# First layer's selective scans: one C product in four on GpSimd, state copies on ScalarE, the D term on TensorE

## The chip, the cores and the metric

The kernel runs on one core of a Trainium2 chip. A core has four compute engines: TensorE (PE in the profile, with its weight loads as PEld), VectorE (DVE), ScalarE (ACT) and GpSimd (POOL). SyncE (SP) computes nothing here; it issues DMA transfers between HBM and the on-chip memory SBUF. TensorE writes its results to PSUM, a second on-chip memory. Each engine runs its own queue in order and waits on semaphores for the others. The metric is the device time of one execution in microseconds, as a median over runs.

## What is computed

A two-layer vision network over 8 images of 128 channels x 64 x 64 positions. The change touches the mixer of the first layer alone. For each image it runs four selective scans ("mamba" blocks), one for each direction d in which the 4096 positions are read. For one direction, cut to what matters:

```python
def step(h, inp):
    x_t, dt_t, B_t, C_t = inp
    dA = jnp.exp(dt_t[..., None] * A)
    h = dA * h + (dt_t * x_t)[..., None] * B_t[:, None, :]
    y = jnp.einsum('bdn,bn->bd', h, C_t)
    return (h, y)
...
y = _selective_scan(xh, dt, A, Bm, Cm) + xh * Dp
y = y * jax.nn.silu(z)
return y @ out_w.T
```

Here h has 128 channels x 16 states. x, dt, B and C are made from the image by a small convolution, a gate and projections; the last two lines add the D term, apply the gate and project out. The four outputs are added to the image. After that come a token router with experts, and a second layer, which the change does not touch.

## The kernel before

**Tiling.** An image's 4096 positions are cut into four chunks of 1024 (`CH`) a direction: 16 chunks an image, 128 in all. The 128 x 16 states do not fit on 128 partitions, so a chunk is worked in 16 blocks (`NQ`): a block holds 8 channels x 16 states on 128 partitions and 1024 positions along the row. `scan_blocks` loops over all blocks n of an image and, in each turn, issues the work of several blocks at different stages:

- `dA` of block n+1: six bf16 matmuls spread dt (in three bf16 parts, tile `parts`) over the states into a PSUM tile (two buffers, tag `dA`); ScalarE turns it into exp(dt A) in place.
- `bx` of block n+1: GpSimd multiplies `xE` (dt x, spread over the states) by `B16`. Three buffers.
- `xE` of block n+3: SyncE issues a DMA which reads 8 rows of `dtx_d`, a copy of dt x in HBM, each row 16 times, and writes 128 partitions x 4 KB, 512 KB in all. Four buffers.
- the scan of block n on VectorE (line 622), from `dA` in PSUM and `bx` in SBUF, written over `dA`; then `hc`, the product with `C16`, on VectorE into SBUF; then the 1-column copy `last`, the state that the same block of the next chunk starts from (not in a direction's last chunk).
- once in four blocks, TensorE adds up the states of the four finished `hc` tiles into `y` in PSUM, half the row in each of two turns ("collects", 4 matmuls each).

**Steps.** What is done once a chunk, rather than once a block, stands in the table at the end of `scan_steps`. A row (at, step, ...) is issued at the end of turn 16 i + at of chunk i: -18 to -2 prepare a chunk while the one before is being scanned, 12 to 20 finish it. Of importance here: `lost` (-9, -8), `ln` and `dt` (-8, -7) make dt; `dtx` (-7, -6) multiplies by x on GpSimd and writes each half row to `dtx_d` by a DMA; `part` and `rest` (-6 to -2) make the three bf16 parts, the `rest` on GpSimd; `z_gate` and `gated` (13 to 16) make the gate `zs`; `skip` (17) adds the D term into `yt` on VectorE; `gate_y` (18, 19) multiplies by the gate on GpSimd, one half row at a time; `out_product` and `out_add` project and add to the image `r`.

**Order.** The helper `ordered` fixes every engine's order as the loop issues it, DMA issues apart: SyncE's order is made by the framework. It comes out as 15 `xE` of a chunk, `dtx` 0, one `xE`, `dtx` 1, then 15 `xE` of the next and so on. An `xE` of a chunk reads both half rows, so the first of them waits until both writes have landed. DMAs issued by SyncE share one queue and start in that order.

Of the kernel before, what the change touches and what calls it, by code (L numbers as in the profile page):

```python
# [9 lines left out]
F32 = mybir.dt.float32  # L10
BF16 = mybir.dt.bfloat16
AF = mybir.ActivationFunctionType
ALU = mybir.AluOpType
# [8 lines left out]
C = 128  # L22
L = 4096
S = 512
# [5 lines left out]
CH = 1024  # L30
# [3 lines left out]
NQ = C // 8  # L34
# [235 lines left out]
def bc(ap, n, axis=None):  # L270

    axis = len(ap.shape) if axis is None else axis
    v = ap.unsqueeze(axis)
    shape = list(v.shape)
    shape[axis] = n
    return v.to_broadcast(shape)


class Net:
# [154 lines left out]
    def scan_steps(self, ch, xp, r, pl, ps):  # L434
# [4 lines left out]
        nc, d, j = self.nc, ch["d"], ch["j"]  # L439
        pool = nc.gpsimd  # L440
# [3 lines left out]
        start = [lo + (1 - q if back else q) * S for q in range(2)]  # L444
        half = [slice(q * S, (q + 1) * S) for q in range(2)]
        ID, TANH = AF.Identity, AF.Tanh
        v = {}
# [4 lines left out]
        def bank(name):  # L452
            p = v[name] = ps.tile([C, S], F32, tag="m", bufs=2, name="m")
            return p

        def make(name, bufs, width=S):
            t = v[name] = pl.tile([C, width], F32, name=name.rstrip("01"), bufs=bufs)
            return t
# [80 lines left out]
                ch[name] = pl.tile([128, CH], F32, name=name, bufs=2)  # L539
            self.ordered(nc.scalar.copy(ch[name][:, half[q]], v[f"b{n}{q}"]))  # L540

        def skip():
            self.stt(make("yt", 1, CH), ch["xs"], self.w(f"D{d}"), ch["y"], ALU.mult, ALU.add)

        def gate_y(q):
            yt = v["yt"][:, half[q]]
            self.tt(yt, yt, v["zs"][:, half[q]], ALU.mult, pool)

        def out_product(q):
            self.mm(bank(f"o{q}"), self.Wo[:, d, :], v["yt"][:, half[q]])  # L550

        def out_add(q):
            p, lo = v[f"o{q}"], CH * j + q * S
# [18 lines left out]
            (-7, spread_copy, 0, 0), (-6, part, 0, 0), (-6, spread_copy, 0, 1), (-5, spread_copy, 1, 0),  # L572
            (-5, spread_copy, 1, 1), (-5, part, 0, 1), (-5, rest, 0, 0), (-4, rest, 0, 1), (-4, part, 1, 0),
            (-4, self.table, EXP_TANH_SET), (-3, part, 1, 1), (-3, rest, 1, 0), (-2, rest, 1, 1),
            (12, z_product, 0), (13, z_product, 1), (13, z_gate, 0), (14, z_gate, 1),
            (15, gated, v, "zs", 0), (16, gated, v, "zs", 1),
            (17, skip), (18, gate_y, 0), (19, gate_y, 1), (19, out_product, 0), (20, out_product, 1),
            (19, out_add, 0), (20, out_add, 1),
        ]
        return table  # L580

    def scan_blocks(self, xp, xt, r, pl, ps):

        nc = self.nc
        chunks = [{"d": d, "j": j} for d in range(4) for j in range(NCH)]
        todo = {}
        for i, ch in enumerate(chunks):  # L590
            for at, step, *args in self.scan_steps(ch, xp if ch["d"] < 2 else xt, r, pl, ps):
                todo.setdefault(NQ * i + at, []).append((step, args))
        total = NQ * len(chunks)
        self.order = {}
        self.table(EXP_TANH_SET)
        xE, bx, dA, hcs = {}, {}, {}, {}
        last = None
        for n in range(min(todo), max(todo) + 1):
            u = n + 1
            if 0 <= u < total:  # L600

                ch, q = chunks[u // NQ], 4 * (u % 4) + u % NQ // 4
                dA[u] = ps.tile([128, CH], F32, tag="dA", bufs=2, name="dA")
                sel = self.expand[:, 8 * q : 8 * q + 8, :].rearrange("p c n -> p (c n)")
                for h in range(2):
                    sg = slice(h * S, (h + 1) * S)
                    for i in range(3):
                        self.mm(dA[u][:, sg], sel, ch["parts"][:, i, sg], start=i == 0, stop=i == 2)
                self.act(dA[u], dA[u], AF.Exp, scale=self.negA[:, ch["d"] * NQ + q : ch["d"] * NQ + q + 1])
                bx[u] = pl.tile([128, CH], F32, name="bx", bufs=3)  # L610
                self.tt(bx[u], xE.pop(u), ch["B16"], ALU.mult, nc.gpsimd)
            u = n + 3
            if 0 <= u < total:
                ch, q = chunks[u // NQ], 4 * (u % 4) + u % NQ // 4
                xE[u] = pl.tile([128, CH], F32, name="xE", bufs=4)
                nc.sync.dma_start(xE[u], bc(ch["dtx"][8 * q : 8 * q + 8, :], NST, 1))
            if 0 <= n < total:
                ch, q = chunks[n // NQ], 4 * (n % 4) + n % NQ // 4
                if n % NQ == 0 and ch["j"] == 0:
                    last = pl.tile([128, NQ], F32, name="last", bufs=2)  # L620
                t = dA.pop(n)
                self.ordered(nc.vector.tensor_tensor_scan(  # L622
                    out=t, data0=t, data1=bx.pop(n), initial=0.0 if ch["j"] == 0 else last[:, q : q + 1],
                    op0=ALU.mult, op1=ALU.add,
                ))
                hcs[n] = pl.tile([128, CH], F32, name="hc", bufs=7)
                self.tt(hcs[n], t, ch["C16"], ALU.mult)
                if ch["j"] < NCH - 1:
                    self.copy(last[:, q : q + 1], t[:, CH - 1 :], nc.vector)
            if n % 4 < 2 and 4 <= n < total + 4:  # L630
                g0, h = n // 4 * 4 - 4, n % 4
                ch, k = chunks[g0 // NQ], g0 % NQ // 4
                if k == 0 and h == 0:
                    ch["y"] = ps.tile([C, CH], F32, tag="y", bufs=1, name="y")
                for g in range(4):
                    self.mm(ch["y"][32 * g : 32 * g + 32, h * S : (h + 1) * S], self.k("collect")[:, 32 * k : 32 * k + 32],
                            hcs[g0 + g][:, h * S : (h + 1) * S], start=k == 0, stop=k == 3)
                    if h:
                        del hcs[g0 + g]
            for step, args in todo.pop(n, ()):  # L640
                step(*args)
        self.order = None
        self.silus_done([])
# [1099 lines left out]
```

## Time and profile before

| | us |
|---|---|
| median of 3 runs | 20,433.81 |
| lowest and highest | 20,432.83 and 20,484.78 |
| span of the profiled execution | 20,491.5 |
| start of the first scan of image 0, of the last of image 7 | 128.8 and 9,602.4 |
| an image's scans, start of the first to start of the last | 1,046 to 1,067 |
| from there to the first scan of the next image | 142 to 145 |
| VectorE, GpSimd, ScalarE busy in 128 to 1,180 | 1,007.75, 815.29, 577.87 |
| TensorE busy in 128 to 1,180 | 791.13 |

The page gives the busy share of every engine over the span; the scans are its first 19 of 40 slices:

```profile
PE   7777677777777777777887888888888888888899
...
DVE  7989899898989989897354666666666666666886
ACT  5555555555555555554353555555555565555553
POOL 6767577676767767675011112112112112111444
...
DMA  4544454454435545444431000000000000001222
```

A digit is the busy share of a slice in tenths; for DMA it is the mean over the core's 16 DMA engines. A group's line in the profile reads: line of the code, engine, operation, tile written <- tiles read, shapes, count | busy us, mean ns of one | idle us of the engine just before them, and what ended it. Many operations have the line of a helper (330 for `tt`, 339 for `stt`, 288 for `mm`, 291 for `act`), so they are told apart by their tiles. In a waits list, "A <- B: us, times, longest" says that A's engine sat idle until B had finished. What bounds the kernel is read off in the prediction.

### The profile page before, as it was taken

What the parts mean: (1) busy time and instruction counts of PE and PEld (TensorE: products, weight loads), DVE (VectorE), ACT (ScalarE), POOL (GpSimd) and SP (SyncE); (2) the same over time, 40 slices, a digit from 0 to 9 for tenths busy, and PEclk for the clock granted to TensorE, in tenths of its full rate; (3) what the DMA queues carried; (4) which work ended last, traced back from release to release, by engine and by line L of the source; (5) the groups of instructions that cost most, each with busy time, mean ns of one, the idle gap of its engine ahead of it and who ended that gap; (6) DMA issues with size and microseconds to landing.
All of it is one profiled execution on the core that took longest, in us unless ns stands there. A gap on an engine that the chain in (4) does not pass through costs nothing. (4 is left out here: it accounts for less than half of the span.)

```text
span 20491.5 us, 295472 instructions
## 1 busy us (share of the span) xinstructions
PE 16535.8 (81%) x111237; PEld 8567.3 (42%) x112221; DVE 15704.4 (77%) x20825; ACT 11194.8 (55%) x15819; POOL 9136.4 (45%) x6292
## 2 busy tenths in 40 slices
PE   7777677777777777777887888888888888888899
PEld 2222222222222222222545666666666666665343
DVE  7989899898989989897354666666666666666886
ACT  5555555555555555554353555555555565555553
POOL 6767577676767767675011112112112112111444
PEclk9989999898999999898687999999999999999899
DMA  4544454454435545444431000000000000001222
GB/s 117 136 106 138 107 136 130 112 135 109 136 108 132 136 109 133 109 132 121 138 124 32 27 26 25 27 25 25 26 26 25 27 26 25 27 25 30 81 97 80
DMA packets 814160, 1684.21 MB, mean 82 GB/s; under 512 B 180859, under 2 KB 413211, under 8 KB 803803
## 3 DMA queue, kind: packets, MB, share of 16 engines
q1 hardware_dynamic: 812734, 1665.25, 29.0%
q8 instruction: 889, 14.57, 0.3%
q14 instruction: 537, 4.40, 0.1%
HBM read 1440.67 MB, written 224.26 MB: 81 GB/s over the span
## 5 line engine op out<-in xcount | busy, mean ns | idle before, releaser
L330 POOL TENSOR_TENSOR bx<-xE,B 128x1024 f32<-128x1024 f32 x2048 | 4819.4, 2354 | 1538.2 <-DMA xE<-dtx_d 1400.7
L288 PE MATMUL dA<-parts,expand 128*128 128x512 bf16 x11816 | 3180.0, 400 | 2124.9 <-DVE last L342 1551.1
L291 ACT ACTIVATE dA<-dA,negA 128x1024 f32<-128x1024 f32 x2048 | 2228.6, 1088 | 3731.3 <-PE dA L288 3647.5
L622 DVE TENSOR_TENSOR_SCAN dA<-dA,last,bx 128x1024 f32<-128x1024 f32 x1536 | 3611.2, 2351 | 209.7 <-POOL bx L330 200.9
L288 PEld LDWEIGHTS <-expand 128*128 128x128 bf16 x12288 | 1078.5, 100 | 4837.7 <-DVE last L342 2739.3
L291 ACT ACTIVATE E_cm<-ss_p 128x1024 f32<-128x1024 f32 x2048 | 1977.1, 1030 | 1545.7 <-PE ss_p L288 674.9
L339 DVE SCALAR_TENSOR_TENSOR E_cm<-E_cm,gm_cm 128x1024 f32<-128x1024 f32 x2048 | 2424.0, 1224 | 512.5 <-ACT E_cm L291 512.1
L330 DVE TENSOR_TENSOR hc<-dA,C 128x1024 f32<-128x1024 f32 x2048 | 2508.0, 1225 | 69.9
L1131 POOL COPY Sd_cm<-S_cm 64x128 f32<-64x128 f32 x1024 | 799.9, 781 | 2886.8 <-DVE S_cm L330 2753.9
L330 POOL TENSOR_TENSOR xD_cm<-tok_cm,D_cm 128x256 f32<-128x256 f32 x512 | 413.8, 808 | 2912.2 <-PE y_p L288 2791.1
L288 PE MATMUL y_p<-E_cm,pad_cm 128*32 128x128 f32 x32768 | 1388.7, 286 | 19.0 <-DVE E_cm L339 10.5
L288 PE MATMUL ss_p<-ssB_cm,ssA_cm 128*128 128x512 bf16 x3584 | 1178.8, 419 | 244.7 <-ACT E_cm L291 167.1
L622 DVE TENSOR_TENSOR_SCAN dA<-dA,bx 128x1024 f32<-128x1024 f32 x512 | 1173.6, 2292 | 197.5 <-POOL bx L330 196.3
L288 PE MATMUL y<-hc,kt 128*32 128x512 f32 x8192 | 1202.0, 652 | 37.8 <-DVE hc L330 31.6
L288 PEld LDWEIGHTS y_p<-E_cm,pad_cm 128*32 128x32 f32 x32768 | 939.4, 113 | 388.6 <-issue 240.7
L288 PE MATMUL bc_p<-stk_cm,W_cm 128*128 128x256 f32 x4096 | 1020.5, 392 | 25.9 <-DMA stk_cm<-xs 20.7
L330 DVE TENSOR_TENSOR gm_cm<-g_p,kt 128x1024 f32<-128x1024 f32 x512 | 624.2, 1219 | 506.3 <-PE g_p L288 501.4
L291 ACT ACTIVATE tok_cm<-tok_p 128x384 f32<-128x384 f32 x1024 | 502.3, 491 | 606.2 <-PE tok_p L288 450.9
L288 PEld LDWEIGHTS bc_p<-stk_cm,W_cm 128*128 128x128 f32 x4096 | 741.0, 191 | 197.0 <-issue 78.8
L291 ACT ACTIVATE BC_cm<-bc_p 128x1024 f32<-128x1024 f32 x512 | 524.9, 1025 | 539.6 <-PE bc_p L288 535.0
L288 PE MATMUL tok_p<-W_cm,stk_cm 128*128 128x200 f32 x4096 | 761.4, 339 | 0.0
L288 PE MATMUL g_p<-BC_cm 64*128 64x128 f32 x8192 | 743.2, 307 | 0.4
(391 smaller groups left out, 30156.3 us busy)
## 6 DMA issues: line engine op xcount, KB each, us to landing
xE<-dtx_d SPq DMA_DIRECT2D x2048, 512.0 KB
dtx_d<-dtx SPq DMA_DIRECT2D x256, 256.0 KB
pb<-p_d SPq DMA_DIRECT2D x64, 1024.0 KB
x<-x SPq DMA_DIRECT2D x192, 256.0 KB
ssA_cm<-cs_cm SPq DMA_DIRECT2D x3072, 4.0 KB
stk_cm<-xs SPq DMA_DIRECT2D x368, 128.0 KB
stk_cm<-y SPq DMA_DIRECT2D x368, 128.0 KB
x<-in_x_dram SPq DMA_DIRECT2D x64, 256.0 KB
```

Source lines behind the costliest of these rows:

```text
L288: self.ordered(self.nc.tensor.matmul(out, lhsT=lhsT, rhs=rhs, start=start, stop=stop))
L291: i = self.ordered(self.nc.scalar.activation(out, in_, func, **kw))
L330: self.ordered((eng or self.nc.vector).tensor_tensor(out, a, b, op))
L339: self.ordered(self.nc.vector.scalar_tensor_tensor(out=out, in0=a, scalar=s, in1=b, op0=op0, op1=op1))
L622: self.ordered(nc.vector.tensor_tensor_scan(out=t, data0=t, data1=bx.pop(n), initial=0.0 if ch["j"] == 0 else last[:, q : q + 1], op0=ALU. ...
L1131: nc.gpsimd.tensor_copy(Sd[gr, :, g * hi : (g + 1) * hi], S2[gr])
```

## The change

- `hc` of blocks 0, 4, 8 and 12 goes to GpSimd: VectorE's scan of block n writes into the SBUF tile `hc` instead of PSUM, and GpSimd multiplies it by `C16` in place in turn n + 1, behind bx of block n + 3.
- `last` is copied by ScalarE, in the scan's turn.
- `bx` is made two blocks ahead instead of one, with four buffers; `xE` is issued four blocks ahead instead of three, still with four buffers.
- The D term becomes eight fp32 matmuls on TensorE, with a diagonal weight `D_diag` (made once a direction), added to `y` in PSUM (16, 17).
- The gate is applied in one VectorE product, `y` in PSUM by `zs` into `zs`, instead of two on GpSimd. `yt` goes. `out_product` and `out_add` come one turn earlier.

In the built program SyncE's order becomes 16 `xE`, both `dtx`, 16 `xE`. On GpSimd the order around turns 9 to 14 becomes bx 11, hc 8, dtx 0, bx 12, dtx 1, bx 13, rest, bx 14, rest, bx 15, hc 12, rest, bx 0 of the next chunk, rest.

```diff
-        def skip():
-            self.stt(make("yt", 1, CH), ch["xs"], self.w(f"D{d}"), ch["y"], ALU.mult, ALU.add)
-
-        def gate_y(q):
-            yt = v["yt"][:, half[q]]
-            self.tt(yt, yt, v["zs"][:, half[q]], ALU.mult, pool)
+        def diagonal():
+            t = self.D_diag = pl.tile([C, C], F32, name="D_diag", bufs=1)
+            self.ts(t, self.k("ident"), self.w(f"D{d}"), ALU.mult)
+
+        def skip(q):
+            for g in range(4):
+                rows_ = slice(32 * g, 32 * g + 32)
+                self.mm(ch["y"][rows_, half[q]], self.D_diag[:, rows_], ch["xs"][:, half[q]], start=False)
+
+        def gate_y():
+            self.tt(v["zs"], ch["y"], v["zs"], ALU.mult)
 
         def out_product(q):
-            self.mm(bank(f"o{q}"), self.Wo[:, d, :], v["yt"][:, half[q]])
+            self.mm(bank(f"o{q}"), self.Wo[:, d, :], v["zs"][:, half[q]])
...
+            *([(12, diagonal)] if j == 0 else []),
             (12, z_product, 0), (13, z_product, 1), (13, z_gate, 0), (14, z_gate, 1),
             (15, gated, v, "zs", 0), (16, gated, v, "zs", 1),
-            (17, skip), (18, gate_y, 0), (19, gate_y, 1), (19, out_product, 0), (20, out_product, 1),
-            (19, out_add, 0), (20, out_add, 1),
+            (16, skip, 0), (17, skip, 1), (17, gate_y), (18, out_product, 0), (19, out_product, 1),
+            (18, out_add, 0), (19, out_add, 1),
...
-                bx[u] = pl.tile([128, CH], F32, name="bx", bufs=3)
-                self.tt(bx[u], xE.pop(u), ch["B16"], ALU.mult, nc.gpsimd)
-            u = n + 3
+            u = n + 2
             if 0 <= u < total:
-                ch, q = chunks[u // NQ], 4 * (u % 4) + u % NQ // 4
+                bx[u] = pl.tile([128, CH], F32, name="bx", bufs=4)
+                self.tt(bx[u], xE.pop(u), where(u)[0]["B16"], ALU.mult, nc.gpsimd)
+            u = n - 1
+            if 0 <= u < total and u % 4 == 0:
+                self.tt(hcs[u], hcs[u], where(u)[0]["C16"], ALU.mult, nc.gpsimd)
+            u = n + 4
+            if 0 <= u < total:
+                ch, q = where(u)
                 xE[u] = pl.tile([128, CH], F32, name="xE", bufs=4)
...
-                t = dA.pop(n)
+                a = dA.pop(n)
+                hcs[n] = pl.tile([128, CH], F32, name="hc", bufs=7)
+                t = a if n % 4 else hcs[n]
                 self.ordered(nc.vector.tensor_tensor_scan(
-                    out=t, data0=t, data1=bx.pop(n), initial=0.0 if ch["j"] == 0 else last[:, q : q + 1],
+                    out=t, data0=a, data1=bx.pop(n), initial=0.0 if ch["j"] == 0 else last[:, q : q + 1],
                     op0=ALU.mult, op1=ALU.add,
                 ))
-                hcs[n] = pl.tile([128, CH], F32, name="hc", bufs=7)
-                self.tt(hcs[n], t, ch["C16"], ALU.mult)
                 if ch["j"] < NCH - 1:
-                    self.copy(last[:, q : q + 1], t[:, CH - 1 :], nc.vector)
+                    self.ordered(nc.scalar.copy(last[:, q : q + 1], t[:, CH - 1 :]))
+                if n % 4:
+                    self.tt(hcs[n], t, ch["C16"], ALU.mult)
...
-                            hcs[g0 + g][:, h * S : (h + 1) * S], start=k == 0, stop=k == 3)
+                            hcs[g0 + g][:, h * S : (h + 1) * S], start=k == 0, stop=False)
```

More of the change, by code (lines that the diff above doesn't have):

```diff
@@ L594, in scan_blocks, with where @@
         self.order = {}
+        def where(u):
+            return chunks[u // NQ], 4 * (u % 4) + u % NQ // 4
         self.table(EXP_TANH_SET)
@@ L609, in scan_blocks @@
                 self.act(dA[u], dA[u], AF.Exp, scale=self.negA[:, ch["d"] * NQ + q : ch["d"] * NQ + q + 1])
-                bx[u] = pl.tile([128, CH], F32, name="bx", bufs=3)
-                self.tt(bx[u], xE.pop(u), ch["B16"], ALU.mult, nc.gpsimd)
-            u = n + 3
+            u = n + 2
             if 0 <= u < total:
-                ch, q = chunks[u // NQ], 4 * (u % 4) + u % NQ // 4
+                bx[u] = pl.tile([128, CH], F32, name="bx", bufs=4)
[5 more added lines that the diff above has]
+            if 0 <= u < total:
+                ch, q = where(u)
                 xE[u] = pl.tile([128, CH], F32, name="xE", bufs=4)
@@ L617, in scan_blocks @@
             if 0 <= n < total:
-                ch, q = chunks[n // NQ], 4 * (n % 4) + n % NQ // 4
+                ch, q = where(n)
                 if n % NQ == 0 and ch["j"] == 0:
                     last = pl.tile([128, NQ], F32, name="last", bufs=2)
-                t = dA.pop(n)
+                a = dA.pop(n)
+                hcs[n] = pl.tile([128, CH], F32, name="hc", bufs=7)
+                t = a if n % 4 else hcs[n]
                 self.ordered(nc.vector.tensor_tensor_scan(
-                    out=t, data0=t, data1=bx.pop(n), initial=0.0 if ch["j"] == 0 else last[:, q : q + 1],
+                    out=t, data0=a, data1=bx.pop(n), initial=0.0 if ch["j"] == 0 else last[:, q : q + 1],
                     op0=ALU.mult, op1=ALU.add,
                 ))
-                hcs[n] = pl.tile([128, CH], F32, name="hc", bufs=7)
-                self.tt(hcs[n], t, ch["C16"], ALU.mult)
                 if ch["j"] < NCH - 1:
-                    self.copy(last[:, q : q + 1], t[:, CH - 1 :], nc.vector)
+                    self.ordered(nc.scalar.copy(last[:, q : q + 1], t[:, CH - 1 :]))
+                if n % 4:
+                    self.tt(hcs[n], t, ch["C16"], ALU.mult)
             if n % 4 < 2 and 4 <= n < total + 4:
```

## The prediction

> **What bounds the kernel now.** The change touches only the scan stage of the first layer: 8 images of 16 chunks of 16 blocks, from 128.8 us to about 9,606 us of the span. I read the page's slices first (VectorE, DVE, at nine tenths there and the DMA engines at half), then the groups, the windows, the order in time of GpSimd (POOL), and the waits.
>
> ```profile
> L330 POOL TENSOR_TENSOR bx<-xE,B 128x1024 f32<-128x1024 f32 x2048 | 4819.4, 2354 | 1538.2 <-DMA xE<-dtx_d 1400.7
> L622 DVE TENSOR_TENSOR_SCAN dA<-dA,last,bx 128x1024 f32<-128x1024 f32 x1536 | 3611.2, 2351 | 209.7 <-POOL bx L330 200.9
> L330 DVE TENSOR_TENSOR hc<-dA,C 128x1024 f32<-128x1024 f32 x2048 | 2508.0, 1225 | 69.9
> ```
>
> VectorE looks like the bound: it idles only some 210 + 198 us before 2048 scans. But look at what GpSimd waits for: the copies xE, 1400.7 us. So to the DMA columns of the windows (last two: share of 16 engines, GB/s):
>
> ```profile
> 264.00:280.00 16.00, 12.75 (x50) 4.07 (x50) 15.86 (x15) 7.05 (x9) 13.80 (x8) 1.00 0.52 125
> 360.00:368.00 8.00, 4.66 (x19) 1.21 (x20) 7.93 (x7) 6.40 (x11) 5.67 (x3) 0.82 0.51 201
> 480.00:488.00 8.00, 6.01 (x25) 1.95 (x27) 7.93 (x8) 4.72 (x6) 7.59 (x5) 1.00 0.52 209
> 320.00:324.00 4.00, 3.93 (x16) 1.56 (x12) 3.96 (x4) 3.73 (x7) 2.59 (x3) 1.00 0.25 70
> ```
>
> The share stands at 0.51 to 0.52 whether 125 or 209 GB/s flow: a resource that is full at one half, whose packets sometimes go slowly, sometimes fast. A copy of 512 KB takes 524,288 B / 125 GB/s = 4.2 us in the one state, 2.5 us in the other. The same in time:
>
> ```profile
> 292.62 2.35 POOL L330 TENSOR_TENSOR bx<-xE,B 128x1024 f32<-128x1024 f32 x1 [1.85 <-DMA xE<-dtx_d]
> 296.82 2.35 POOL L330 TENSOR_TENSOR bx<-xE,B 128x1024 f32<-128x1024 f32 x1 [1.86 <-DMA xE<-dtx_d]
> 301.01 2.35 POOL L330 TENSOR_TENSOR bx<-xE,B 128x1024 f32<-128x1024 f32 x1 [1.84 <-DMA xE<-dtx_d]
> ...
> 329.48 2.37 POOL L330 TENSOR_TENSOR bx<-xE,B 128x1024 f32<-128x1024 f32 x1 [3.41 <-DMA xE<-dtx_d]
> ```
> ```profile
> 361.30 2.34 POOL L330 TENSOR_TENSOR bx<-xE,B 128x1024 f32<-128x1024 f32 x1 [0.32 <-DMA xE<-dtx_d]
> 363.93 2.35 POOL L330 TENSOR_TENSOR bx<-xE,B 128x1024 f32<-128x1024 f32 x1 [0.28 <-DVE hc L330]
> 370.01 1.26 POOL L330 TENSOR_TENSOR dtx<-dt,xs 128x512 f32<-128x512 f32 x1 [3.73 <-DVE dt L330]
> ```
>
> In the first, products start 4.20 us apart and each waits for its copy: the DMA paces all. The 3.41 us is a chunk's first copy, which cannot be issued before both writes of dtx have landed. In the second, GpSimd has caught up and stands at VectorE. So the stage swings between two limits. From the trace's DMA packets (128 of 4 KB a copy), chunk by chunk over all 128: a chunk takes 66.55 us on average (scan to scan, image ends apart); its 16 copies span 63.8, then come 2.7 idle to the next chunk's first packet. In only 29 chunks did the copies run out of buffers, because the engines were late. With those 29 closed up (copies after the stall at 2.6 us), I estimate 62.5 + 2.7 = 65.2 us a chunk for a DMA queue that nobody holds up. This is the floor.
>
> **What the Trainium skill says.** "DMA: Bandwidth & Descriptors", section "Why a DMA increments its semaphore by 16 and not by 1": a DMA is spread over as many engines as divide its slowest dimension, at most 16. Source of xE: 8 rows, each repeated 16 times; so 8 engines. The share of 0.51 agrees. "SBUF — State Buffer", "Two separate sides": compute cannot slow a DMA; agrees in that both rates occur with DVE above 90% busy. So no edit here speeds the copies. "Who interferes with whom" there: a VectorE instruction with one SBUF input does not contend with GpSimd. The changed ones (scan, gate_y) have the other in PSUM, and bx in the trace takes 2.35 us beside every VectorE operation; I keep all prices. "GPSIMD Engine Reference", "Elementwise": a two-input product costs GpSimd about twice VectorE's time; here 2354 to 1225 ns.
>
> **The change, part by part, for one chunk.** Durations overlap at their ends, so on VectorE I use start to start in its order of time (483.97, 486.35, 487.50, 487.56): scan 2.38, hc 1.14 to 1.15, last 0.07.
> VectorE before: 16 x (2.38 + 1.14 + 0.07) = 57.4; lost, m, dt twice each (0.60 + 0.72 + 0.61) = 3.9; yt 1.2; out_add 1.2 (2.0 or more where strided). Sum 63.7; chunks at this limit do take 62.7 to 64.5.
> - Four hc to GpSimd: -4 x 1.14 = -4.6.
> - last to ScalarE: -0.8. It costs ScalarE 12 x some 0.2 (as its 128x4 activation at 6.16 us) = 2.4; ScalarE is 55% busy. But the copy waits for the scan, and behind it in ScalarE's order stand the steps (plus_one, ln) which used to run during the scan.
> - yt to TensorE, and the gate from two GpSimd products to one VectorE product from PSUM: yt 1.18 against about 1.14: 0. TensorE gains 8 matmuls, 2 x 1.06 us (the price of four collects, each in two passes).
> - Bare sum -5.4: 58.3. New waits, each followed through the queues from one scan's end S: after a block whose C product is on GpSimd, VectorE goes straight to the next scan, but dA for it comes at S + 1.2 (hc) + 1.5 (six matmuls) + 1.1 (exp) + latencies = 3.95 against 3.55: 0.4, three or four times. In block 8 (no hc) lost waits for plus_one behind last: 1.5. gate_y in block 1 waits for dA, four collects and four skips on TensorE: 1.7. So -5.4 + 3.6 = -1.8: VectorE's chunk about 61.9 (bounds 58.3 and 63.7).
> - GpSimd: before 16 x 2.35 + 12 halves (10 + 2 gate_y) = about 52. After +4 x 2.35 - 2 x 1.23: 58.9. Also under the floor, but dense: blocks 9 to 14 carry six bx, two hc, two dtx and four rest, 25.8 us against 6 x 4.2 of DMA.
> - bx two ahead with four buffers, xE issued a block earlier with the same four: a copy still follows the release by bx of four blocks before, so the DMA's backlog (some 8 us, two copies) is the same. What moves is on SyncE: all 16 copies now precede both dtx writes, and dtx 1 comes behind bx 12 and hc 8 instead of bx 11 on GpSimd, some 6 us later against the copies. With copies at 4.2 us it is issued 7 us before copy 15 ends: hidden. Where the last four run at 2.5, the chunk's gap grows by about 2.1 us; I count this for one chunk in eight, 0.25 us.
> - Image ends: one block of steps less, gate in one product: -2 us, 8 times, -16.
>
> Sum. An infinitely fast consumer would give 66.55 - 65.2 = 1.35 us a chunk. VectorE at 61.9 instead of 63.7 gives about half of it: a chunk whose copies need 61 wins two thirds of its loss, one whose copies need 58 wins a third. -0.7 + 0.25 = -0.45 us, x 128 = -58, and -16: -74 us, on an execution of 20,491.5 us (the profiled one; the median of the runs shown is 57.7 lower). On the median 20,433.8: 20,360 us, -0.36%.
>
> **The rivals.**
> 1. The copies free of the engines: all of 1.35 is won, 128 x 1.35 + 16 = -189: 20,245. For it: VectorE's bare sum of 58.3. Against: the waits just counted.
> 2. VectorE bounds after all and -5.4 goes through: -691 - 16: 19,727. For it: its 0.9 busy. Against: share of 0.51 throughout.
> 3. No gain: the gap's growth of 2.1 us hits one chunk in three (0.7) and eats the win. Then only the -16 is left: 20,418.
> 4. Slower: the hold of the first copy by dtx. If GpSimd runs behind in blocks 9 to 14 (it has 0.9 us too much work there, and its hc waits for VectorE), dtx 1 is issued after copy 15 has ended, and every microsecond is DMA idle time. It decides from 7 us of lag at 4.2 us a copy, at once at 2.5. At 2 us in each chunk: +256, less the -74: 20,616.
> That the scans wait for PE's eight new matmuls, or bx 0 before the last rest delays the first dA (3 us once a chunk), is covered by the bx buffers while the DMA paces.
>
> **How the numbers follow.** Forecast 0.50, rival 1 0.15, rival 2 0.03, rival 3 0.17, rival 4 0.15. About 0.3% (61 us) is what a measurement can tell from no change; the three runs before differ by 52. Of the forecast's own range, 20,290 to 20,430, I put six tenths beyond -0.3%. Faster 0.30 + 0.15 + 0.03 = 0.48; same 0.20 + 0.17 = 0.37; slower 0.15. The range 20,230 to 20,520 leaves out rival 2, a little of rival 1 and most of rival 4.
>
> **What would show it.** Right: DMA share still 0.50 over an image's scans, GpSimd still waiting for xE, VectorE busy some 107 us less an image (16 x (4 x 1.225 + 12 x 0.148)) but idle in its place (more waits for bx, for sp_u and for y), hc on GpSimd at 2.35 us. Wrong: a mean packet rate that changed, products on VectorE or GpSimd that got longer, or SyncE waiting longer for dtx than the 976 us of before between 300 and 9,000 us.

## The result, and the profile after

| | before | after |
|---|---|---|
| median, same chip, 4 runs each | 20,435.16 us | 20,630.67 us |
| lowest to highest | 20,432.83 to 20,484.78 | 20,620.78 to 20,637.51 |
| span of the profiled execution | 20,491.5 us | 20,619.0 us |
| first scan of image 0 to last scan of image 7 | 9,473.6 us | 9,620.3 us |

The changed kernel is slower: ratio 1.0097, 95% interval 1.0081 to 1.0112, where 0.9964 was forecast. The profiled execution of before lies at the upper end of its runs, so the two spans differ by 127.5 us and the medians by 195.5; comparisons below use ratios of runs, and the profiles for the mechanism.

The same groups as shown of before, now of the changed kernel (128 to 9,790 us of the span):

```profile
L330 POOL TENSOR_TENSOR bx<-xE,B 128x1024 f32<-128x1024 f32 x2048 | 4811.4, 2354 | 833.4 <-DMA xE<-dtx_d 772.7 <-DVE dA L639 15.5 <-DVE hc L330 15.5
L639 DVE TENSOR_TENSOR_SCAN dA<-dA,last,bx 128x1024 f32<-128x1024 f32 x1152 | 2708.3, 2351 | 152.3 <-ACT last L644 105.1 <-ACT dA L291 44.2 <-POOL bx L330 2.9
L330 DVE TENSOR_TENSOR hc<-dA,C 128x1024 f32<-128x1024 f32 x1536 | 1881.1, 1225 | 775.0 <-ACT last L644 762.3
L330 POOL TENSOR_TENSOR hc<-hc,C 128x1024 f32<-128x1024 f32 x512 | 1208.2, 2360 | 93.6 <-ACT last L644 79.1 <-DVE hc L639 12.4 <-DMA xE<-dtx_d 1.8
```

No operation got dearer: bx still 2354 ns, the scan 2351, hc 1225 on VectorE and 2360 on GpSimd. GpSimd waits for copies half as long (772.7 us for 1400.7 us): the DMA paces less. What is new is in the third line. The C product used to follow its scan with 69.9 us of idle time in all; now 762.3 us pass, 1152 times, until ScalarE has copied `last`. The order in time of VectorE shows one block after another:

```profile
458.89 1.23 DVE L330 TENSOR_TENSOR hc<-dA,C 128x1024 f32<-128x1024 f32 x1 [0.23 <-ACT last L644]
460.03 2.29 DVE L639 TENSOR_TENSOR_SCAN dA<-dA,bx 128x1024 f32<-128x1024 f32 x1
462.89 1.23 DVE L330 TENSOR_TENSOR hc<-dA,C 128x1024 f32<-128x1024 f32 x1 [0.57 <-ACT last L644]
464.03 2.29 DVE L639 TENSOR_TENSOR_SCAN dA<-dA,bx 128x1024 f32<-128x1024 f32 x1
466.88 1.23 DVE L330 TENSOR_TENSOR hc<-dA,C 128x1024 f32<-128x1024 f32 x1 [0.57 <-ACT last L644]
```

and the same stretch of ScalarE why:

```profile
461.68 1.09 ACT L291 ACTIVATE dA<-dA,negA 128x1024 f32<-128x1024 f32 x1 [0.57 <-PE dA L288]
462.69 0.16 ACT L644 COPY last<-dA 128x1 f32<-128x1 f32 x1
...
465.67 1.09 ACT L291 ACTIVATE dA<-dA,negA 128x1024 f32<-128x1024 f32 x1 [1.09 <-PE dA L288]
466.69 0.16 ACT L644 COPY last<-dA 128x1 f32<-128x1 f32 x1
```

`last` of block n stands in ScalarE's order behind the exponential of block n + 1. That exponential waits for TensorE's matmuls, and these for the PSUM buffer that hc of block n - 1 frees. So a loop closes: hc (n - 1), matmuls, exponential (n + 1), `last` (n), hc (n). hc starts at 458.89, 462.89 and 466.88: the loop takes 4.0 us a block, more than a scan and a product, 2.29 + 1.14.

Every one of the 1152 hc that follow such a copy waits for ScalarE, although both only read the tile. The Trainium skill gives the reason in "PSUM — Partial Sum Buffer", section "PSUM bank collisions raise a hardware error": no two of the engines may touch the same part of a PSUM bank at once, reads against reads included, and a compiler's scheduler therefore orders them. This agrees with the waits here; that an access without a turn goes wrong no run shows. Readers of a tile in SBUF are not ordered in this way: the C products of GpSimd and of VectorE in one chunk, which both read `C`, overlap in time in 231 of 512 cases of the changed kernel.

From the starts of the scans in the trace I took the length of each chunk (block 0 to block 0 of the next, image ends apart), by its place in a direction. Chunk 3, a direction's last, copies no `last`. The last column is the time from a chunk's last copy packet to the next chunk's first.

```
us       chunk 0     1     2     3    mean    gap
before      67.4  67.1  66.0  65.5   66.55   2.66
after       70.0  69.1  68.3  63.6   68.01   3.94
```

The chunks with `last` lose 2 to 2.6 us, the chunk without it gains 1.9. But the gap has grown too. Two theories follow. **Theory A**: the wait of hc for `last` is the loss, and the wider gap is mostly its consequence. **Theory B**, the prediction's rival 4: SyncE's new order (both dtx writes behind all 16 copies) widens the gap, and that is the loss; its 20,616 us lies nearest to the result.

### The profile page after: what moved, and what is told of

The parts are those of the page before. It is cut to its first block, busy times and chain, and to the rows that moved or that the text cites. A ratio compares the mean times of both kernels' runs of the same rounds, so it can differ in the third digit from the quotient of the medians.

```text
span 20619.0 us, 299312 instructions
## 1 busy us (share of the span) xinstructions
PE 16869.4 (82%) x114269; PEld 8714.2 (42%) x114269; DVE 15012.1 (73%) x18809; ACT 11330.1 (55%) x17355; POOL 9980.2 (48%) x6548
## 3 DMA queue, kind: packets, MB, share of 16 engines
q1 hardware_dynamic: 812734, 1665.25, 29.2%
## 5 line engine op out<-in xcount | busy, mean ns | idle before, releaser
L330 POOL TENSOR_TENSOR bx<-xE,B 128x1024 f32<-128x1024 f32 x2048 | 4811.4, 2354 | 833.4 <-DMA xE<-dtx_d 772.7
L288 PE MATMUL dA<-parts,expand 128*128 128x512 bf16 x12288 | 3264.9, 404 | 1932.6 <-DVE hc L330 1721.7
L288 PEld LDWEIGHTS <-expand 128*128 128x128 bf16 x12288 | 1125.2, 101 | 4538.0 <-DVE hc L330 2687.8
L639 DVE TENSOR_TENSOR_SCAN dA<-dA,last,bx 128x1024 f32<-128x1024 f32 x1152 | 2708.3, 2351 | 152.3 <-ACT last L644 105.1
L330 DVE TENSOR_TENSOR hc<-dA,C 128x1024 f32<-128x1024 f32 x1536 | 1881.1, 1225 | 775.0 <-ACT last L644 762.3
L288 PE MATMUL ss_p<-ssB_cm,ssA_cm 128*128 128x512 bf16 x4096 | 1240.3, 419 | 188.2 <-ACT E_cm L291 167.0
L330 POOL TENSOR_TENSOR hc<-hc,C 128x1024 f32<-128x1024 f32 x512 | 1208.2, 2360 | 93.6 <-ACT last L644 79.1
L639 DVE TENSOR_TENSOR_SCAN dA<-dA,bx 128x1024 f32<-128x1024 f32 x384 | 879.2, 2290 | 63.4 <-ACT last L644 63.3
L639 DVE TENSOR_TENSOR_SCAN hc<-dA,last,bx 128x1024 f32<-128x1024 f32 x384 | 899.2, 2342 | 2.8 <-ACT dA L291 2.4
```

The lines of the kernel that those rows point to most:

```text
L288: self.ordered(self.nc.tensor.matmul(out, lhsT=lhsT, rhs=rhs, start=start, stop=stop))
L330: self.ordered((eng or self.nc.vector).tensor_tensor(out, a, b, op))
L639: self.ordered(nc.vector.tensor_tensor_scan(out=t, data0=a, data1=bx.pop(n), initial=0.0 if ch["j"] == 0 else last[:, q : q + 1], op0=ALU. ...
```

## The experiments

Ratios are to the kernel before, run on the same chip each time, with the 95% interval. The times expected in us were set from the 20,435 us above; on the chip of e1 to e4 the kernel before takes 20,387 us, so ratios are the fairer comparison.

**`e1_last_split`: the copy back on VectorE where the tile is in PSUM.**

```diff
-                if ch["j"] < NCH - 1:
-                    self.ordered(nc.scalar.copy(last[:, q : q + 1], t[:, CH - 1 :]))
                 if n % 4:
                     self.tt(hcs[n], t, ch["C16"], ALU.mult)
+                if ch["j"] < NCH - 1:
+                    if n % 4:
+                        self.copy(last[:, q : q + 1], t[:, CH - 1 :], nc.vector)
+                    else:
+                        self.ordered(nc.scalar.copy(last[:, q : q + 1], t[:, CH - 1 :]))
```

> The changed kernel, but the last state of the twelve blocks a chunk that stay in PSUM is copied by VectorE again, behind its C product; the four blocks whose scan goes to SBUF keep ScalarE's copy. Everything else of the change stays (bx two blocks ahead, the four C products on GpSimd, the D term on TensorE, the gate from PSUM). Theory A (the copy on ScalarE makes the C product wait, and nothing else of the change costs much): the three chunks of a direction that copy last states fall from 69.1 us to about 65 us, as the fourth (63.6) plus VectorE's own copies (0.8), and the time is 20,200 to 20,380, below the kernel before. Theory B (the gap between the copies of two chunks, 1.28 us wider, comes from SyncE's new order and is the cause by itself): the time stays at 20,550 or more. The prediction's own floor (copies at 65.2 us a chunk) would give 20,360.

Measured: 20,420.89 us, ratio 1.0015 (1.0006 to 1.0024); chunks 67.2, 65.9, 66.0, 65.1, mean 66.10; gap 3.73. The loss is gone, against theory B. The gain that theory A promised did not come: the ratio is above 1. And the gap stayed wide, so it is no mere consequence of the wait. Something other than `last` holds this kernel at 66 us; the later experiments look for it. The ratio has a limit here. In the profiles e1's scans are 81 us shorter than those of before (9,392.4 for 9,473.6 us), but that execution of before lies at the upper end of its runs, and the part behind the scans, which no edit touches, took 24 us longer (10,913.0 for 10,889.1). Over all profiles that part takes 10,852 to 10,913 us, so a ratio of whole executions can be off by up to 0.3% as a measure of the scans.

**`e2_last_on_ACT_alone`: the kernel before with this one edit.**

```diff
-                self.tt(hcs[n], t, ch["C16"], ALU.mult)
                 if ch["j"] < NCH - 1:
-                    self.copy(last[:, q : q + 1], t[:, CH - 1 :], nc.vector)
+                    self.ordered(nc.scalar.copy(last[:, q : q + 1], t[:, CH - 1 :]))
+                self.tt(hcs[n], t, ch["C16"], ALU.mult)
```

> The kernel before with one edit: the last state is copied by ScalarE, issued ahead of the C product. Theory A: all sixteen C products of a chunk wait behind ScalarE's copy, some 0.4 us each as in the changed kernel, so a chunk that copies gets 3 to 5 us longer and the time is 20,700 to 20,950; waits of hc for ScalarE's last of over 1,000 us appear in the list of waits. Theory B: SyncE's order is that of before, so the time stays within 60 us of 20,435.

Measured: 20,666.82 us, ratio 1.0134 (1.0119 to 1.0149); chunks 69.2, 69.6, 69.5, 63.9; gap 2.69, as before. In its list of waits:

```profile
DVE hc L330 <- ACT last L628: 673.8, 1536, 1.8
```

The wait is shorter than the 1,000 us expected. The time lies just under the range, but 1.0134 on 20,435 us would be 20,709, inside it. The edit alone makes the kernel slower, with SyncE's order and the gap untouched. Theory B cannot explain this. Nor can the clock granted to TensorE: its mean over the profiled execution is 0.921 before and 0.914 in the changed kernel, but 0.926 here, where the time is longer, and 0.911 in e1, where the loss is gone.

**`e3_last_behind_hc`: the changed kernel, with ScalarE's copy issued behind hc.**

```diff
-                if ch["j"] < NCH - 1:
-                    self.ordered(nc.scalar.copy(last[:, q : q + 1], t[:, CH - 1 :]))
                 if n % 4:
                     self.tt(hcs[n], t, ch["C16"], ALU.mult)
+                if ch["j"] < NCH - 1:
+                    self.ordered(nc.scalar.copy(last[:, q : q + 1], t[:, CH - 1 :]))
```

> The changed kernel with two statements swapped: ScalarE's copy of the last state is issued behind VectorE's C product instead of ahead of it; both still read the same PSUM tile. Theory A: the C product no longer waits for ScalarE; the copy waits for the C product, which is spare time there; 20,180 to 20,350 us and less than 100 us of hc waiting for last. If ScalarE's place (the copy in its order between two exponentials) and not the order of the two readers were what costs, it would stay near 20,630. Theory B: 20,550 or more.

Measured: 20,541.33 us, ratio 1.0075 (1.006 to 1.009): a clear miss for theory A. The time is just under what B would give, and the ratio (20,588 on 20,435 us) within it. It is 0.2% less than with the copy ahead, but the two intervals touch. Its waits:

```profile
ACT last L646 <- DVE hc L330: 1162.8, 860, 4.1
PE dA L288 <- ACT last L646: 1053.1, 791, 2.8
```

hc waits no longer, but the wait has turned round: ScalarE stands 1162.8 us until hc is done, with its exponentials and steps queued behind, and TensorE waits for `last`, now the last reader, before it may overwrite the buffer. So it is not only the order of the two readers that costs: against e1, on the same chip, the copy on ScalarE still costs 0.6%. A second engine as a reader of that PSUM tile puts one more hand-over into the loop, and here it cost in both orders.

**`e4_wide_copies_before`: is the copies' rate the floor of before?**

```diff
-                ch["dtx"] = self.dp.tile([C, CH], F32, name="dtx_d", bufs=2)
+                ch["dtx"] = self.dp.tile([C, 2, CH], F32, name="dtx_d", bufs=2)
...
-            nc.sync.dma_start(ch["dtx"][:, half[q]], t)
+            nc.sync.dma_start(ch["dtx"][:, :, half[q]], bc(t, 2, 1))
...
-                nc.sync.dma_start(xE[u], bc(ch["dtx"][8 * q : 8 * q + 8, :], NST, 1))
+                nc.sync.dma_start(xE[u], bc(ch["dtx"][8 * q : 8 * q + 8].rearrange("c t n -> (c t) n"), NST // 2, 1))
```

> The kernel before, with dt*x written to DRAM twice side by side, so that each spreading copy reads 16 source rows (each sent to 8 partitions) instead of 8 (each to 16). If the copies' rate on the 8 DMA engines that they use is the floor of a chunk in the kernel before, as the prediction took it: the DMA share spreads over 16 engines, a copy takes well under 4 us, VectorE's 63.7 us a chunk become the bound, and the time is 20,100 to 20,250. If the rate isn't the floor: 20,435 within 60 us.

Measured: 20,127.67 us, ratio 0.9867 (0.985 to 0.9883); mean chunk 63.75 us, in directions 0 and 1 chunks 1 and 2 take 63.8 us on average, in 2 and 3, where out_add is strided, 64.9. The scans' wait for bx, 200.9 us in the same group of the kernel before, is gone, and GpSimd now waits for VectorE:

```profile
L330 POOL TENSOR_TENSOR bx<-xE,B 128x1024 f32<-128x1024 f32 x2048 | 4815.4, 2355 | 448.9 <-DVE dA L622 444.2 <-DMA xE<-dtx_d 1.3
L622 DVE TENSOR_TENSOR_SCAN dA<-dA,last,bx 128x1024 f32<-128x1024 f32 x1536 | 3608.8, 2349 | 6.3 <-ACT dA L291 6.1
```

So the copies were a floor, as the prediction said, and under it lies VectorE's chunk: 63.75 us, for the 63.7 that it added up. If the DMA queue also holds e1 at 66 us, is it by its rate or by its gap? The next two ask this.

**`e5_order_last_split` and `e6_order_last_ACT`: SyncE's order, with `last` as in e1 and as in the changed kernel.** The edit is the same in both; in SyncE's order dtx 0 then stands ahead of copy 14 of a chunk and dtx 1 ahead of copy 15.

```diff
-            nc.sync.dma_start(ch["dtx"][:, half[q]], t)
+            self.ordered(nc.sync.dma_start(ch["dtx"][:, half[q]], t))
...
-                nc.sync.dma_start(xE[u], bc(ch["dtx"][8 * q : 8 * q + 8, :], NST, 1))
+                self.ordered(nc.sync.dma_start(xE[u], bc(ch["dtx"][8 * q : 8 * q + 8, :], NST, 1)))
```

> As e1_last_split (ratio 1.0015 to before), with one more edit: SyncE's DMAs keep the loop's order, so both writes of dtx of the next chunk stand ahead of the copies 14 and 15 of this one (before: ahead of 15 and behind it; changed kernel: both behind all 16). Theory C (what e1 still lacks is lost in the gap between two chunks' copies, 3.7 us there, because both writes of dtx queue behind the last copy and the next chunk's first copy waits for them): the gap falls under 1 us, a chunk from 66.1 to 63 or 63.5 us, where VectorE bounds it, and the ratio to 0.978 to 0.985. Theory D (the gap doesn't matter, the engines of the changed kernel are simply no faster than 66 us): within 0.3% of e1.

> The changed kernel with SyncE's order alone changed in the same way; the last state stays on ScalarE ahead of the C product. Theory A (the wait of the C product for ScalarE's copy bounds VectorE at about 67 us a chunk in three chunks of four): the gap falls here too, but a chunk that copies stays at 67 to 68.5 us, only the fourth gets a little faster, and the ratio stays at 1.000 to 1.008. Theory B (the wider gap is the cause of the loss): ratio 0.98 to 0.99, as the order removes the whole gap.

Measured: e5 20,302.8 us, ratio 0.9948 (0.9929 to 0.9967), mean chunk 65.17; e6 20,522.18 us, ratio 1.0056 (1.004 to 1.0072), chunks 69.0, 68.2, 68.0, 62.9. The gap at the chunk's end is closed in both (-0.2 us). e6 is theory A's picture: with no gap left, chunks with `last` stay at 68. Theory C is right in its direction, worth 0.67%, and wrong in size by more than half: the stall moved inside the chunk. From copy 13 to copy 14, behind dtx 0, it is 6.67 us from start to start where e1 has 3.58; idle time of the queue, gap and inside together, only fell from 3.8 to 2.6 us a chunk. And the copies' rate stays.

**`e7_wide_last_DVE` and `e8_wide_last_ACT`: the change with the DMA out of the way.** Both are the changed kernel with e4's copies; e7 has in addition

```diff
-                if ch["j"] < NCH - 1:
-                    self.ordered(nc.scalar.copy(last[:, q : q + 1], t[:, CH - 1 :]))
                 if n % 4:
                     self.tt(hcs[n], t, ch["C16"], ALU.mult)
+                if ch["j"] < NCH - 1:
+                    self.copy(last[:, q : q + 1], t[:, CH - 1 :], nc.vector)
```

> The changed kernel with all last states copied by VectorE behind the C product, and with dt*x written twice side by side so that a copy reads 16 rows, as in e4 (0.9867 to before). The copies then bound nothing, and what the change is worth to VectorE alone shows against e4: if its 16 x 1.2 us of products, four of them moved away, give what the prediction worked out (61.9 + 0.8 for last against 63.7), a chunk takes 62 to 62.7 us and the ratio is 0.979 to 0.983; if the bare sum of 59 us goes through, 0.965; if new waits eat it, 0.986 as e4.

> The changed kernel with the copies of 16 rows alone. Theory A: with the copies out of the way the chunks that copy last states stay bound by the loop C product, matmul, exponential, last state, at 66.6 to 67.5 us, the fourth falls to 61.5: ratio 0.996 to 1.003, little better than the changed kernel's 1.0097 and far above e4's 0.9867. Theory B, or any cause on the DMA side: 0.985 or below.

Measured: e7 20,024.7 us, ratio 0.9813 (0.9798 to 0.9828), chunks 63.5, 63.4, 63.3, 61.9; e8 20,478.46 us, ratio 1.0037 (1.0022 to 1.0052), chunks 67.8, 68.3, 67.9, 62.2. e7 has the ratio expected, e8 lies just above its range. GpSimd waits for copies only 5.1 and 8.9 us in all, so DMA is no limit here, and SyncE's order is the same in both. This settles A against B: `last` on ScalarE costs 1.0037 - 0.9813 = 2.24%, and the kernel is slower than before. In e8 hc waits for it as in the changed kernel:

```profile
DVE hc L330 <- ACT last L644: 687.2, 1152, 1.9
```

The order in time of VectorE in e7 shows the waits that the prediction had counted, in blocks 8, 12 and 1:

```profile
538.07 2.34 DVE L639 TENSOR_TENSOR_SCAN hc<-dA,last,bx 128x1024 f32<-128x1024 f32 x1
540.45 0.15 DVE L342 COPY last<-hc 128x1 f32<-128x1 f32 x1
542.25 0.70 DVE L339 SCALAR_TENSOR_TENSOR m<-sp_u,m 128x512 f32<-128x512 f32 x1 [1.65 <-ACT sp_u L291]
...
559.12 2.36 DVE L639 TENSOR_TENSOR_SCAN dA<-dA,last,bx 128x1024 f32<-128x1024 f32 x1 [0.31 <-ACT dA L291]
...
577.71 1.22 DVE L330 TENSOR_TENSOR zs<-y,zs 128x1024 f32<-128x1024 f32 x1 [1.35 <-PE y L288]
```

**`e9_wide_D_part`: the D term and the gate alone, on e4.** The edit is the upper half of the change's diff (`diagonal`, `skip`, `gate_y`, `out_product`, the table, `stop=False`).

> The kernel before with the copies of 16 rows (e4, 0.9867) and one part of the change: the D term on TensorE and the gate as one product from PSUM on VectorE. In the prediction this part trades 1.2 us for 1.2 us on VectorE and adds a wait of 1.7 us a chunk for TensorE in block 1, and GpSimd's two products go. If so, a chunk takes 1.2 to 1.7 us more than in e4, and D_diag, which takes some 1.5 us of VectorE beside GpSimd's work, adds 50 us: ratio 0.994 to 1.000. If the gate's wait is hidden (the block's C product still stands ahead of it here): 0.986 to 0.990.

Measured: 20,252.58 us, ratio 0.9903 (0.9885 to 0.9921), mean chunk 64.76, 1.0 us above e4. The ratio lies between the two forecasts. The gate waits, but less than the 1.7 us a chunk expected: 115.5 us in all, 45 of them at the eight image ends.

```profile
L330 DVE TENSOR_TENSOR zs<-y,zs 128x1024 f32<-128x1024 f32 x128 | 156.8, 1225 | 115.5 <-PE y L288 115.5
```

So this part loses 0.36% (0.9903 for e4's 0.9867) when VectorE is the bound. The rest of the change without `last` (C products, bx two ahead) brings the other way 0.9813 against 0.9903, 0.9%; bx two ahead was not tried apart from the C products.

**`e10_gate_later` and `e11_C_on_block_2`: from e7, the waits taken out.** e10:

```diff
-            self.ts(t, self.k("ident"), self.w(f"D{d}"), ALU.mult)
+            self.act(t, self.k("ident"), ID, scale=self.w(f"D{d}"))
...
-            (16, skip, 0), (17, skip, 1), (17, gate_y), (18, out_product, 0), (19, out_product, 1),
-            (18, out_add, 0), (19, out_add, 1),
+            (16, skip, 0), (17, skip, 1), (18, gate_y), (19, out_product, 0), (20, out_product, 1),
+            (19, out_add, 0), (20, out_add, 1),
```

> As e7_wide_last_DVE (0.9813), with the gate's product one turn later (18 instead of 17, out_product and out_add one turn later too), when TensorE has finished y, and D_diag made by ScalarE. If the waits counted are real: the 198 us in which the gate waits for y go, and 32 times 1.6 us of D_diag, so 0.969 to 0.974. If VectorE just waits elsewhere instead: above 0.978.

e11, on top of it (and `u % 4 == 2` for GpSimd's product):

```diff
-                t = a if n % 4 else hcs[n]
+                t = hcs[n] if n % 4 == 2 else a
...
-                if n % 4:
+                if n % 4 != 2:
                     self.tt(hcs[n], t, ch["C16"], ALU.mult)
```

> As e10_gate_later, with GpSimd's C products those of blocks 2, 6, 10 and 14 instead of 0, 4, 8 and 12, so that the block in whose turn VectorE waits for sp_u (8) has its C product on VectorE again. If that wait (270 us in e7 over the scans, 144 in e4) was caused by the missing product, it falls by 100 us or more and the ratio is 0.963 to 0.970. Against it: the collects of TensorE come one turn after GpSimd's product instead of three, so PE waits for hc; if that reaches the scans, no gain over e10 or a loss.

Measured: e10 19,976.52 us, ratio 0.977 (0.9749 to 0.9792); e11 19,883.37 us, ratio 0.9724 (0.9706 to 0.9742), the fastest version tried, mean chunk 61.84. Both gained, but less than expected, and e10's interval reaches the 0.978 that was to mean that VectorE just waits elsewhere. The waits, first two of e10, then the same two of e11:

```profile
DVE m L339 <- ACT sp_u L291: 257.1, 134, 16.1
...
DVE dA L639 <- ACT dA L291: 175.1, 337, 3.2
```
```profile
DVE dA L639 <- ACT dA L291: 326.4, 452, 14.7
...
DVE m L339 <- ACT sp_u L291: 151.0, 54, 15.8
```

The wait for sp_u falls by 106 us, as expected, and the scans' wait for the exponential grows by 151: part of each wait removed comes back one step on. Of the gate's 198 us in e7, 47 and 35 are left, in eight waits, one at each image's end: inside the images the wait is gone.

## Why the prediction was wrong

**The step that failed** is "last to ScalarE: -0.8", with its price "12 x some 0.2" on ScalarE. It followed what stands behind the copy in ScalarE's order, and not what on VectorE waits for the copy: hc, queued right behind the scan and reading the same PSUM tile. It also missed that `last` stands behind the next exponential. Instead of saving 0.8 us a chunk on VectorE the step costs, by e8 against e7, 66.81 - 63.08 = 3.7 us a chunk on average where the copies do not bound, and 68.01 - 66.10 = 1.9 with the copies as they are. By the runs it is 1.0097 - 1.0015, 0.82% or 168 us: most of the 195. (In the profiles the scans differ by 228 us, and the part behind them by 47 the other way.) The prediction drew on the skill's rules for SBUF ports; the rule for PSUM named above, from which the wait follows, it did not use.

**The DMA floor.** That the copies set one was right (e4). Its height, 65.2 us, no run measured.

**VectorE's chunk** of before, 63.7, was right. The new one came out right but for `last`, and in part by luck. The sum has a slip: the waits make 3.6 only if the 0.4 counts once, while the text says three or four times. Counted so they make 4.4 to 4.8, and the chunk 62.7 to 63.1 instead of 61.9. In e7 the three waits take, per chunk, 0.93 us for the exponential (119.1 over 128 chunks), 0.99 more than in e4 for sp_u (270.2 less 143.5) and 1.55 for the gate (198.0): 3.5 together, each of the last two smaller than counted and the first larger than a single 0.4. With the 0.8 of `last` put back, 61.9 becomes 62.7; in e7 chunks 1 and 2 of directions 0 and 1 take 62.7 on average (63.8 in e4), and the chunk without `last` 61.4, 61.6 in e8. Over all chunks, though, e7 gains only 0.67 us on e4 (63.08 for 63.75) where this sum has 1.0: a direction's first chunk takes 63.5 for 62.7. `D_diag`, below, stands in that chunk.

**The gap's growth** was too small by a factor of four or five: 0.25 us a chunk, measured 1.28 in the changed kernel and 1.07 in e1. The prediction charged only dtx 1 that comes late (one chunk in eight). In the trace it is late, issued less than 1 us before copy 15 ends or after it, in 36% of the chunks, with a gap of 5.1 us; but the chunks in which it is early also have 3.3 instead of 2.7. e5, which puts both writes ahead of the last copy and has no gap, shows that the order is the cause. SyncE's queue shows the same shift, first in the kernel before, then in the changed one (300 to 9,000 us):

```profile
SPq L616 <- DMA dtx_d<-dtx: 976.3, 149, 13.5
SPq L521 <- POOL dtx L330: 557.5, 234, 21.5
```
```profile
SPq L521 <- POOL dtx L330: 1027.6, 230, 21.8
...
SPq L631 <- DMA dtx_d<-dtx: 471.5, 127, 8.4
```

The prediction named a longer wait for dtx_d as a sign of trouble. That wait halved; the trouble is in the other line, SyncE's wait for GpSimd's dtx, which doubled. Rival 4 thus had its mechanism in part and its time by accident.

The prediction also held that bx two ahead leaves the copies' backlog as it was, and so missed a gain. In the kernel before the queue stands still inside a chunk too, 0.52 us on average, and 30 of the 32 stalls over 0.3 us come ahead of copy 15: its buffer is freed by bx 11, which GpSimd works behind dtx 0. With bx two ahead, bx 11 comes before dtx 0, and 0.07 us of stall are left, in the changed kernel and in e1. Gap and stalls together grow from 3.18 us a chunk to 4.01 in the changed kernel and 3.80 in e1.

With the gap of e1 in place of the 0.25, the forecast's sum without `last` is -0.45 + 0.82 = +0.37 us a chunk, or 47 us for 128; e1's ratio says 31 us. The agreement proves little: this sum leaves out the change in the stalls, and the chunk means of the two profiles differ by -0.45, though that of before lies at the upper end of its runs (all runs of before, on all chips, spread over 178 us). That the gain and the wider gap just about cancel is thus worked out, not shown by a run of its own; that SyncE's order in e5 gives 0.67% is shown.

**The image ends** were to give 2 us each; from the last scan to the next image's first it is 144.8 us for 143.9 before. The gate waits 5.3 us for TensorE there in the changed kernel, where the D term waited 3.1 to 3.7 before. Whether that took the gain is not shown: in e9 the gate waits 5.1 to 6.6 us there, and the image end takes 141.2.

**D_diag** had no price at all, and it is missing from the operations of the change that the prediction held against GpSimd (scan, gate_y). It takes VectorE 1.53 us on average:

```profile
L334 DVE TENSOR_SCALAR D_diag<-kt,w_first 128x128 f32<-128x128 f32 x32 | 48.9, 1527 | 0.0
```

## What to carry to other kernels

Before giving a small copy to an idle engine, list the readers of its source tile. Here a second engine's read of a PSUM tile took its turn with the first engine's, and since it stood behind an instruction that depended on the first, a 0.16 us copy closed a loop. Count for each moved instruction both what is queued behind it and what waits for it elsewhere. When a stage has two limits close to each other, widen one (as e4 does) and measure the edits there: what they are worth shows only then. The wide copies, the change without `last` on ScalarE and the two shifts of e10 and e11 together gave 2.8%, where the change alone lost 1%.

## What the runs showed that was not expected

The time of a copy depended on how many source rows it reads. In the kernel before, copies of 8 rows, each read 16 times, follow each other at 3.6 to 4.2 us on average, by their place in the chunk (copy 15 apart). With the source written twice, so that 16 rows are read 8 times each, they follow at 2.0 to 2.4 us where nothing holds them up (e7), and the DMA share over 530 to 668 us is 0.60 where it stood at 0.52. That took the copies off the critical path although more bytes move (1732.42 MB for 1665.25 in the queue). Why the copies of 8 rows ran at two rates, 125 and 209 GB/s at the same share, no run here shows.

A VectorE tensor_scalar from SBUF to SBUF can stand until GpSimd's running product ends. All engines of the changed kernel in order of time, D_diag and what runs on GpSimd beside it:

```profile
454.03 2.35 POOL L330 TENSOR_TENSOR bx<-xE,B 128x1024 f32<-128x1024 f32 x1
454.15 2.31 DVE L334 TENSOR_SCALAR D_diag<-kt,w_first 128x128 f32<-128x128 f32 x1
```

It ends at 456.46, bx at 456.38; 30 of the 32 end within 0.1 us after the GpSimd operation beside which they began. The shortest of the 32, which began after one had ended, takes 0.26 us, the median 1.81, and the same on ScalarE 0.39 (e10). "SBUF — State Buffer", section "Who interferes with whom", in the Trainium skill names tensor_scalar among the operations that can take the port pair shared with GpSimd and says that the later one then blocks fully; the ends of the two agree. Two-input products of VectorE with one input in PSUM kept their 1225 ns beside GpSimd throughout.
